# Score banks in pairs with one maximum per pair, the other products in four banks, and a planner that issues value sums and whole-array products in separate steps

## The chip, the core and the metric

The kernel runs on one core of one Trainium2 chip. The metric is the device time of one execution in microseconds. Three runs of the kernel before gave 1620.12, 1620.18 and 1624.03 us, median 1620.18 us. Engines are called PE (matrix products; PEld is its weight load), DVE (vector), ACT (activation), POOL (GpSimd) and SP (which here only issues DMAs).

## The reference

Input `x` is 32 sequences of 256 rows of 128 numbers. Each sequence goes through a pre-norm decoder layer and then a mixture-of-experts layer. The change lies in the attention of the decoder layer alone, so that is what must be seen:

```python
x = layer_norm(hidden_states, ln1_g, ln1_b)
q, k, v = jnp.split(x @ c_attn_w + c_attn_b, 3, axis=-1)
a = _attn_core(split_heads(q), split_heads(k), split_heads(v), causal_bool=True)      # 16 heads of 8
hidden_states = merge_heads(a) @ attn_proj_w + attn_proj_b + residual
x = layer_norm(hidden_states, lnx_g, lnx_b)
q = x @ q_attn_w + q_attn_b                                  # keys and values from the encoder rows
a = _attn_core(..., extra_bias=scorer_logits, tril_diag2_additive=True)
hidden_states = hidden_states + merge_heads(a) @ x_proj_w + x_proj_b
# then layer norm, a gelu MLP, layer norms with residuals, gate, 8 experts with top 2, a shared expert
```

`_attn_core` is softmax(q k / sqrt(8) + mask) v, with the row maximum subtracted.

## The kernel before, in words

There are 32 self attentions (s0 to s31) and 32 cross attentions (c0 to c31), one of each for every sequence. A head has only 8 numbers, so the scores are made in strips of 32 rows of the array: four groups g of four heads j, the group's operands in partitions 32g to 32g+31, and a number of q or k in three bf16 parts. Four matmuls, one for each strip, run at once, into four PSUM banks.

One attention has these pieces:

- `normed_in`: layer norm. For a self attention the input is normalised twice, to `xn` (which is multiplied later) and to `hs`, the residual in `h_all`; `moments` and both `normed` are DVE work, `rsqrt` (L190, L191) is POOL work.
- `turned`, `projections`, `values`: whole-array products with float32 operands. `projected` (L240) splits q and k into bf16 parts on POOL (L250 to L253), writes them to DRAM and reads them back in strip order (tiles `q`, `k`, then `qs`, `kr`), on the SP queue.
- `maxima` (L420): scores by query into banks `sc`, a quarter of the array rows each; DVE takes the negative maximum of each bank (L443). Its only purpose is the row maximum. `split` (POOL) makes three bf16 parts of the maxima, `turned_maxima` transposes them.
- `weights` (L477): scores by key, once more, with the maximum added as a product, into banks `st`; ACT takes exp to the tile `wt` (L503).
- `weighted` (L513): value sums `av`, which use 32 columns of the array at a time (128*32 in the profile); 64 matmul passes for most of them.
- `back`, `turned_back`, `joined`: transposes and the output product, whole-array again.

The order on PE is written out by hand. Time is counted in half steps. A self attention takes 6 half steps by query and 6 by key, a cross attention 8 and 8; the keys start LAG = 13 half steps after the queries. A planner in the kernel's Python places each attention, and each extra piece at a half step. Then a loop goes through pairs of half steps (called a step below): `issue` mixes the score products of the step by query and by key over the four strips, then come the maxima and exps, then the extras of the step, with `weighted` last. Thus PE does a block of score products, then the extras, then the next block. Within a block the first half fills `sc` of two groups and `st` of the other two, the second half the reverse. The order of the other engines is left to a scheduler at build time.

All PSUM tiles come from one ring of eight banks (tag `ps`, L159 to L162): a step's four `sc`, four `st` and its extras in turn. A product waits until the bank that it gets was read: an `sc` bank by DVE's maximum, an `st` bank by ACT's exp, an extra's bank by its copy.

The planner's function `full(step, cost, ...)` puts a piece at a step, or one later when the step has more than 1.9 of cost; `weighted` goes through it too, so a step may hold value sums and whole-array products. AHEAD = 7 bounds how many self attentions may run ahead of the cross attentions. After attention come a stage of norms and MLP and the experts' stage, with the same ring of eight banks.

Of the kernel before, what the change touches and what calls it, by code (L numbers as in the profile page):

```python
# [27 lines left out]
LAG = 13  # L28
V_BUFS = 4
QK_BUFS = 4  # L30
AHEAD = 7


COLS = ["ln1_g", "ln1_b", "lnx_g", "lnx_b", "ln2_g", "ln2_b", "bq", "bk", "bqx", "bkx", "bv", "bvx"]
# [10 lines left out]
def transformer_moe_kernel(ctx: ExitStack, tc: tile.TileContext, ins, out: bass.AP):  # L45
# [152 lines left out]


    with ExitStack() as actx:  # L200
        wk = actx.enter_context(tc.tile_pool(name="wk", bufs=3))
        wl = actx.enter_context(tc.tile_pool(name="wl", bufs=5))
        wtp = actx.enter_context(tc.tile_pool(name="wtp", bufs=22))
        kx = actx.enter_context(tc.tile_pool(name="kx", bufs=1))
        dram = actx.enter_context(tc.tile_pool(name="dram", bufs=1, space=bass.MemoryType.DRAM))

# [135 lines left out]
        class Attention:  # L342
# [77 lines left out]
            def maxima(self, qb, js, gp):  # L420

                nk = S if qb else (P + 2 if self.cross else P)
                n = len(js)
                if qb not in self.ms:
                    self.ms[qb] = wl.tile([P, NG, NJ], F32, tag="m", name="m")
                m = self.ms[qb]
                work, tiles = {}, []
                for g in (2 * gp, 2 * gp + 1):
                    st = slice(32 * g, 32 * g + 32)
                    t3 = bank("sc")[:, 0 : n * nk].rearrange("p (c k) -> p c k", k=nk)  # L430
                    tiles.append((g, t3))
                    todo = [(nk, t3[:, c, :], self.qs[st, j, qb * P : qb * P + P], self.kr[st, j, part, 0:nk],
                             (c, part) == (0, 0)) for c, j in enumerate(js) for part in range(3)]
                    for a in range(5 if self.cross and not qb else 4):
                        k0 = qb * P + 32 * a
                        w = min(32, nk - k0)
                        todo.append((n * w, t3[:, :, k0 : k0 + w], eye_q[self.cross][st, a, :],
                                     tri_q[st, 0:w].unsqueeze(1).to_broadcast([32, n, w]), False))
                    work[g] = todo

                def after():
                    for g, t3 in tiles:
                        nc.vector.tensor_reduce(m[:, g, js[0] : js[0] + n], t3, AX.X, ALU.max, negate=True)  # L443
                return work, after

            def split(self, qb):
# [10 lines left out]
            def turned_maxima(self, qb):  # L457
                if qb == 0:
                    self.mT = wl.tile([P, S], BF16, tag="mT", name="mT")
                pt = ps.tile([P, P], BF16, tag="ps", name="pt_m")  # L460
# [16 lines left out]
            def weights(self, kb, js, gp):  # L477
# [107 lines left out]
        extra, filled = {}, {}  # L585

        def on(step, f, *args):
            extra.setdefault(step, []).append((f, args))

        def full(step, cost, f, *args):  # L590
# [4 lines left out]
            filled[e] = filled.get(e, 0) + cost  # L595
            on(e, f, *args)
            return e

        by_query, by_key, first, free = {}, {}, {}, {}
        at = begun = ended = 0
        cross = True
        while ended < NB:
            ready = ended < begun and first[ended] <= at
            cross = begun == NB or (ready and not cross) or begun - ended == AHEAD
            if cross:
                x = pairs[ended][1]
                at = max(at, first[ended])
                ended += 1  # L610
            else:
                x = pairs[begun][0]
                begun += 1

            at = max(at, *(free.get((x.cross, what, x.b % n), at) for what, n in (("qk", QK_BUFS), ("v", V_BUFS))))
            at += at % 2
            halves, keys = x.query_halves(), x.key_halves()
            s = at
            at += len(halves)
            if not x.cross:  # L620
                on(s - 22, x.load)
            on(s - 18, x.normed_in)
            if x.b < QK_BUFS:
                on(s - 17, x.spares)
            on(s + 2, x.biased)
            e = full(s - 14, 0.35, x.turned)
            e = full(e + 2, 0.5 if x.cross else 0.9, x.projections)
            assert e <= s - 8, (e, s)
            if not x.cross:
                full(e + 2, 0.55, x.values)  # L630
            for i, h in enumerate(halves):
                by_query[s + i] = (x, h)
            for qb in range(2):
                last = s + max(i for i, h in enumerate(halves) if h[0] == qb)
                on(last + 1, x.split, qb)
                e = full(last + 3, 0.13, x.turned_maxima, qb)
                assert e < s + LAG
            for i, h in enumerate(keys):
                by_key[s + LAG + i] = (x, h)
            end = s + LAG + len(keys)  # L640
            free[x.cross, "qk", x.b % QK_BUFS] = end + 14
            half = end if x.cross else s + LAG + sum(h[0] == 0 for h in keys)
            e = full(half + 1, 1.2 if x.cross else 0.9, x.weighted, 0)
            e = full(max(e, end + 1), 1.8, x.weighted, 1)
            free[x.cross, "v", x.b % V_BUFS] = e + 12
            e = full(e + 2, 0.5, x.back)
            e = full(e + 2, 0.25, x.turned_back)
            e = full(e + 2, 0.6, x.joined)
            first[x.b] = e + 20

        on(-18, spares)
        on(-15, diagonals)
        on(-13, max_frames, False)
        on(-11, picks)
        on(-9, out_biases)
        full(-5, 0.5, encoder_turned)
        on(-5, logit_parts)
        on(-4, encoder_rows)
        full(-2, 0.5, encoder_keys)
        full(0, 0.5, encoder_values)  # L660
        on(2, max_frames, True)
# [254 lines left out]

    def experts(c):
        rhs = xnT[:, c * CH * P : (c + 1) * CH * P]
        pw = ps.tile([P, P], BF16, tag="ps", name="pw")
# [98 lines left out]
```

## Time and profile before

One execution was profiled: its own time was 1619.44 us, with a span of 1617.7 us, so 1.7 us lie around the span.

| stretch of the span, us | what runs | PE busy, us | DVE busy, us | ACT busy, us | POOL busy, us | granted PE clock |
|---|---|---|---|---|---|---|
| 0 to 200 | start of attention | 134.4 | 121.7 | 78.2 | 104.7 | 0.85 |
| 200 to 960 | attention, steady | 677.6 | 535.4 | 486.2 | 346.8 | 0.99 |
| 960 to 1016 | end of attention | 47.8 | 27.4 | 32.8 | 10.7 | 0.98 |
| 1016 to 1204 | norms and MLP | 171.0 | 130.8 | 121.9 | 114.2 | 0.91 |
| 1204 to 1617.7 | experts | 405.0 | 231.8 | 93.7 | 39.7 | 0.99 |

Attention takes 63% of the span. The first block of scores starts at 34.7 us and the last attention product ends near 1014 us. A row of the profile's groups names the line, engine, operation and tiles, how often it ran, the total busy time, the mean of one in ns, and the idle time of the engine before it with what ended that idle time. "issue" there means that nothing that the profile shows ended it. A float32 matmul is two passes, and each counts as a matmul and a weight load.

### The profile page before, as it was taken

Reading aid. Unit: us, or ns where it says so; the run is one execution under the profiler, and the core shown is the slowest. Engines: PE = TensorE matmul, PEld = TensorE weight load, DVE = VectorE, ACT = ScalarE, POOL = GpSimd, SP = SyncE. Lnnn points to the kernel's source line nnn. Section 1 sums busy time; section 2 is a strip of 40 time slices with the busy share of each in tenths; the row PEclk is TensorE's granted clock in tenths of the full one; section 3 lists DMA queues with packets and bytes.
Section 4 is the critical chain, followed back from the end, with each engine's and each line's share of the span. In section 5 each row is a group of like instructions: output and inputs, shape, how many; then the busy total and the mean of one; then the engine's idle time right before and its main releaser. Section 6 shows DMA issues by size and latency. Waiting matters only on the chain.

```text
span 1617.7 us, 74346 instructions
## 1 busy us (share of the span) xinstructions
PE 1435.8 (89%) x33116; PEld 1110.6 (69%) x33116; DVE 1047.0 (65%) x2749; ACT 812.7 (50%) x1824; POOL 616.1 (38%) x1443
## 2 busy tenths in 40 slices
PE   3677898998889888889898998799889999999997
PEld 2566677777777777777777777477655656565665
DVE  6647677676676776777666664477766464646564
ACT  1353566666666666666666565678532222222221
POOL 7444445444454444544444231687511010100101
PEclk8888899999999999999999999899979999999999
DMA  5632233232322322313232010600000000000000
GB/s 135 188 100 75 63 92 97 77 112 65 104 86 74 109 70 86 104 61 111 68 90 89 28 32 11 163 1 1 1 1 13 7 13 7 14 7 14 7 14 13
DMA packets 106033, 97.25 MB, mean 60 GB/s; under 512 B 4764, under 2 KB 105360, under 8 KB 105712
## 3 DMA queue, kind: packets, MB, share of 16 engines
q1 hardware_dynamic: 104432, 91.49, 18.4%
q8 instruction: 259, 4.24, 1.1%
q10 hardware_dynamic: 1280, 1.01, 0.2%
q14 instruction: 62, 0.51, 0.1%
HBM read 54.47 MB, written 37.77 MB: 57 GB/s over the span
## 4 chain that ended last, share of the span: by engine, by line
PE 68%; DVE 17%; POOL 5%; ACT 4%; issue 3%; DMA 2%; SPq 0%; POOLq 0%; ACTq 0%; DVEq 0%
DVE m L443 11%; PE av L525 11%; PE sc L580 9%; PE po L944 8%; PE pa L930 8%; PE pb L931 8%; PE st L580 7%; PE po L853 4%; PE pf L846 3%; PE pq L245 3%; ACT wt L503 2%; POOL r L191 2%; PE pc L937 2%; DVE st L182 2%; PE pa L541 1%
## 5 line engine op out<-in xcount | busy, mean ns | idle before, releaser
L443 DVE TENSOR_REDUCE m<-sc 128x2 f32<-128x512 f32 (+2 forms) x896 | 496.3, 608 | 236.9 <-PE sc L580 215.0
L503 ACT ACTIVATE wt<-st 128x512 f32<-128x512 f32 (+1 forms) x896 | 420.7, 539 | 256.3 <-PE st L580 196.8
L580 PEld LDWEIGHTS <-qs 32*128 32x128 bf16 x6144 | 225.2, 95 | 93.7 <-issue 80.5
L933 ACT ACTIVATE sa<-pa,cols 128x512 f32<-128x512 f32 x144 | 98.9, 687 | 308.5 <-PE pa L930 305.7
L580 PE MATMUL st<-mT,pick 32*128 32x256 bf16 (+2 forms) x2048 | 241.4, 244 | 5.1 <-issue 5.1
L190 POOL TENSOR_SCALAR r<-mv 128x2 f32<-128x2 f32 (+1 forms) x160 | 31.9, 199 | 501.9 <-DVE mv L183 434.3
L580 PEld LDWEIGHTS <-strips 32*128 32x128 bf16 x7424 | 189.3, 94 | 22.3 <-issue 18.8
L580 PE MATMUL sc<-kr,qs 32*128 32x128 bf16 (+1 forms) x3072 | 164.5, 250 | 33.3 <-DMA kr<-k 25.0
L580 PE MATMUL st<-qs,kr 32*128 32x128 bf16 (+1 forms) x3072 | 177.8, 247 | 10.2 <-issue 6.1
L580 PE MATMUL sc<-krx,qs 32*128 32x256 bf16 (+1 forms) x3072 | 178.9, 246 | 5.4 <-issue 3.5
L580 PE MATMUL st<-qs,krx 32*128 32x130 bf16 (+1 forms) x3072 | 176.7, 243 | 4.8 <-issue 3.5
L930 PE MATMUL pa<-h_all,w 128*128 128x512 f32 x288 | 149.4, 601 | 0.0
L931 PE MATMUL pb<-h_all,w 128*128 128x512 f32 x288 | 147.9, 595 | 0.0
L580 PE MATMUL sc<-strips 32*128 32x64 bf16 (+2 forms) x3840 | 140.3, 193 | 6.2 <-issue 5.8
L580 PE MATMUL st<-strips 32*128 32x64 bf16 (+2 forms) x3584 | 136.3, 192 | 9.1 <-issue 8.9
L944 PE MATMUL po<-w,h 128*128 128x128 f32 x1152 | 141.6, 277 | 0.0
L944 PEld LDWEIGHTS po<-w,h 128*128 128x128 f32 x1152 | 134.9, 192 | 7.7 <-issue 7.7
L525 PE MATMUL av<-wt,vpadx 128*32 128x128 f32 (+1 forms) x4096 | 111.7, 253 | 31.9 <-DVE m L443 28.2
L191 POOL TENSOR_TENSOR r<-r,nhalf 128x2 f32<-128x2 f32 (+1 forms) x160 | 133.2, 838 | 9.9
L580 PEld LDWEIGHTS <-kr 32*128 32x128 bf16 x3072 | 117.0, 94 | 19.1 <-issue 16.5
L525 PEld LDWEIGHTS av<-wt,vpadx 128*32 128x32 f32 x4096 | 98.3, 112 | 43.9 <-DVE m L443 36.2
L934 DVE SCALAR_TENSOR_TENSOR h<-pb,cols,sa 128x512 f32<-128x512 f32 x144 | 107.7, 749 | 31.9 <-PE pb L931 28.2
(163 smaller groups left out, 2624.5 us busy)
## 6 DMA issues: line engine op xcount, KB each, us to landing
kr<-k SPq DMA_DIRECT2D x32, 768.0 KB
k<-qkp SPq DMA_DIRECT2D x32, 576.0 KB
qs<-q SPq DMA_DIRECT2D x64, 256.0 KB
q<-qkp SPq DMA_DIRECT2D x64, 192.0 KB
x<-in_x_dram SPq DMA_DIRECT2D x32, 128.0 KB
x_all<-in_x_dram SPq DMA_DIRECT2D x8, 512.0 KB
out_dram<-y SPq DMA_DIRECT2D x16, 256.0 KB
w<-in_rw_dram SPq DMA_DIRECT2D x1, 1024.0 KB
```

The costliest lines, as they stand in the source:

```text
L191: nc.gpsimd.tensor_tensor(r, r, nhalf[:, 0:n], ALU.pow)
L245: nc.tensor.matmul(pq[:, i * S : i * S + S], lhsT=w, rhs=xT, start=True, stop=True)
L443: nc.vector.tensor_reduce(m[:, g, js[0] : js[0] + n], t3, AX.X, ALU.max, negate=True)
L503: nc.scalar.activation(w[:, 0 : n * nq], t, AF.Exp)
L525: nc.tensor.matmul(av[32 * g : 32 * g + 32, j // 2, to : to + n], lhsT=self.vp[:, kb, g, WINDOW[j] : WINDOW[j] + 32], rhs=self.wts[kb, g, ...
L580: nc.tensor.matmul(dst, lhsT=lhsT, rhs=rhs, start=start, stop=False, skip_group_check=True)
L853: nc.tensor.matmul(po[:, i, :], lhsT=self.g[:, f, i * P : (i + 1) * P], rhs=wmlp[:, f, :], start=f == 0, stop=f == FF // P - 1)
L930: nc.tensor.matmul(pa, lhsT=w1[:, e, 0:D], rhs=rhs, start=True, stop=True)
L931: nc.tensor.matmul(pb, lhsT=w1[:, e, D : 2 * D], rhs=rhs, start=True, stop=True)
L933: nc.scalar.activation(sa, pa, AF.Silu, bias=col(C_B1 + 2 * e))
L934: nc.vector.scalar_tensor_tensor(h[:, e, :], pb, col(C_B1 + 2 * e + 1), sa, ALU.add, ALU.mult)
L944: nc.tensor.matmul(po[:, i, :], lhsT=h[:, e, i * P : (i + 1) * P], rhs=w2[:, e, :], start=e == 0, stop=False)
```

## The change

- **Banks.** In attention, two rings take the place of one: `sc` tiles are now pairs of banks, two pairs in all (four banks), and everything else (`st`, `av`, transposes, projections) shares four banks. A ring of eight is opened again after attention.
- **Maximum.** One DVE maximum reads a pair (two groups) where two read one bank each: 448 operations for 896.
- **Norm of a self attention.** The two reciprocal roots are made in one power operation of four columns on POOL where two had two columns each; the residual `hs` is normalised on POOL, not DVE.
- **Exp tiles.** The ring of 22 tiles of 512 columns becomes 18 of 512 and 8 of 260.
- **Planner.** `full` now chooses the cheapest of several steps within a reach; a step that holds a value sum is dear to it, and value sums are placed by `columns` without regard to cost. The plan is made four times, each time with the last round's value-sum steps. AHEAD is 8, preparation begins 28 and 24 half steps ahead for 22 and 18, and buffers count as free sooner.

The diff, cut to its core:

```diff
-AHEAD = 7
+AHEAD = 8
+SOON = 2
...
-    ps = ctx.enter_context(tc.tile_pool(name="ps", bufs=8, space=PSUM))
-    def bank(name):
-        return ps.tile([P, 512], F32, tag="ps", name=name)
+    rings = {}
+    def bank(name, dtype=F32, n=512):
+        return rings["ps"].tile([P, n], dtype, tag="ps", name=name)
...
+        rings["sc"] = actx.enter_context(tc.tile_pool(name="ps_sc", bufs=2, space=PSUM))
+        rings["ps"] = actx.enter_context(tc.tile_pool(name="ps_a", bufs=4, space=PSUM))
-        wtp = actx.enter_context(tc.tile_pool(name="wtp", bufs=22))
+        wtp = actx.enter_context(tc.tile_pool(name="wtp", bufs=1))
...
-                    r1 = rsqrt(wk, mv, 1.0, EPS, "a")
-                    r2 = rsqrt(wk, mv, 1.0 + EPS, EPS * EPS, "b")
+                    r = wk.tile([P, 2, 2], F32, tag="rab", name="r")
+                    nc.gpsimd.tensor_scalar(r[:, 1, :], mv[:, :, 1], 1.0 + EPS, EPS * EPS, ALU.mult, ALU.add)
+                    nc.gpsimd.tensor_scalar(r[:, 0, :], mv[:, :, 1], 1.0, EPS, ALU.mult, ALU.add)
+                    nc.gpsimd.tensor_tensor(r, r, nhalf.rearrange("p (a b) -> p a b", b=2), ALU.pow)
+                    r1, r2 = r[:, 0, :], r[:, 1, :]
                     for t in range(2):
                         normed(self.xn[:, t, :], xs[t], mv, r2, t)
-                        normed(self.hs[t], xs[t], mv, r1, t)
+                        nc.gpsimd.tensor_scalar(self.hs[t], xs[t], mv[:, t, 0:1], r1[:, t : t + 1],
+                                                ALU.subtract, ALU.mult)
...
+                t4 = rings["sc"].tile([P, 2, 512], F32, tag="sc", name="sc")[:, :, 0 : n * nk].rearrange(
+                    "p g (c k) -> p g c k", k=nk)
                 for g in (2 * gp, 2 * gp + 1):
-                    t3 = bank("sc")[:, 0 : n * nk].rearrange("p (c k) -> p c k", k=nk)
+                    t3 = t4[:, g % 2]
...
-                    for g, t3 in tiles:
-                        nc.vector.tensor_reduce(m[:, g, js[0] : js[0] + n], t3, AX.X, ALU.max, negate=True)
+                    nc.vector.tensor_reduce(m[:, 2 * gp : 2 * gp + 2, js[0] : js[0] + n], t4, AX.X, ALU.max, negate=True)
...
-                        w = wtp.tile([P, 512], F32, tag="wt", name="wt")
+                        cols, bufs = (512, 18) if n * nq > 260 else (260, 8)
+                        w = wtp.tile([P, cols], F32, tag=f"wt{cols}", name="wt", bufs=bufs)
...
-            e = step + step % 2
-            if filled.get(e, 0) + cost > 1.9 and filled.get(e + 2, 0) < filled.get(e, 0):
-                e += 2
+                def price(e):
+                    return max(0, filled.get(e, 0) + cost - 2.3) + 0.5 * (e in taken) + 0.02 * (e - step)
+                e = min(range(step + step % 2, max(step + step % 2, step + reach) + 1, 2), key=price)
...
+            def columns(step, f, *args):
+                e = step + step % 2
+                own.add(e)
+                on(e, f, *args)
+                return e
...
-            at = max(at, *(free.get((x.cross, what, x.b % n), at) for what, n in (("qk", QK_BUFS), ("v", V_BUFS))))
+                at = max(at, free.get(qk, -99) + 10)
...
-            free[x.cross, "qk", x.b % QK_BUFS] = end + 14
+                free[qk] = end + 1
-            e = full(half + 1, 1.2 if x.cross else 0.9, x.weighted, 0)
-            e = full(max(e, end + 1), 1.8, x.weighted, 1)
+                e = columns(half + 1, x.weighted, 0)
+                e = columns(max(e + 2, end + 1), x.weighted, 1)
...
-            first[x.b] = e + 20
+                first[x.b] = e + (26 if x.b >= SOON else 16)
...
+    rings["ps"] = ctx.enter_context(tc.tile_pool(name="ps", bufs=8, space=PSUM))
```

In the steady part the plan repeats every 14 half steps (seven steps, one self and one cross attention). Before, the seven steps hold: four steps with one value sum each, three of these with whole-array products ahead of it (`turned`; `back`, two `turned_maxima` and `projections`; `turned_back`), and three steps with whole-array products alone. After, four steps hold one value sum each (one of these with a `turned_maxima`), and three hold all else: step A two `back`, two `turned_maxima`, `values` and `turned`; step B two `turned_back`, `projections` of a cross attention and `turned`; step C two `joined`, a `turned_maxima` and `projections` of a self attention. Over the whole plan, 90 steps mix a value sum with whole-array products before and 36 after.

More of the change, by code (lines that the diff above doesn't have):

```diff
@@ L426, in maxima @@
                 m = self.ms[qb]
-                work, tiles = {}, []
+                work = {}
+                t4 = rings["sc"].tile([P, 2, 512], F32, tag="sc", name="sc")[:, :, 0 : n * nk].rearrange(
+                    "p g (c k) -> p g c k", k=nk)
                 for g in (2 * gp, 2 * gp + 1):
                     st = slice(32 * g, 32 * g + 32)
-                    t3 = bank("sc")[:, 0 : n * nk].rearrange("p (c k) -> p c k", k=nk)
-                    tiles.append((g, t3))
+                    t3 = t4[:, g % 2]
                     todo = [(nk, t3[:, c, :], self.qs[st, j, qb * P : qb * P + P], self.kr[st, j, part, 0:nk],
@@ L459, in turned_maxima @@
                     self.mT = wl.tile([P, S], BF16, tag="mT", name="mT")
-                pt = ps.tile([P, P], BF16, tag="ps", name="pt_m")
+                pt = bank("pt_m", BF16, P)
                 nc.tensor.transpose(pt, self.mp[qb].rearrange("p g r -> p (g r)"), ident_b)
@@ L584, in transformer_moe_kernel @@
         pairs = [(Attention(b, False), Attention(b, True)) for b in range(NB)]
[L585 to L590, printed above, removed]
-            e = step + step % 2
-            if filled.get(e, 0) + cost > 1.9 and filled.get(e + 2, 0) < filled.get(e, 0):
-                e += 2
[L595 to L613, printed above, removed]
-            at = max(at, *(free.get((x.cross, what, x.b % n), at) for what, n in (("qk", QK_BUFS), ("v", V_BUFS))))
[L616 to L640, printed above, removed]
-            free[x.cross, "qk", x.b % QK_BUFS] = end + 14
-            half = end if x.cross else s + LAG + sum(h[0] == 0 for h in keys)
-            e = full(half + 1, 1.2 if x.cross else 0.9, x.weighted, 0)
-            e = full(max(e, end + 1), 1.8, x.weighted, 1)
[L645 to L648, printed above, removed]
-            first[x.b] = e + 20
@@ L651, in transformer_moe_kernel, with planned, on, full @@
[L651 to L661, printed above, removed]
+        def planned(taken):
+            extra, filled, by_query, by_key, first, joined, free = {}, {}, {}, {}, {}, {}, {}
+            def on(step, f, *args):
+                extra.setdefault(step, []).append((f, args))
+            def full(step, cost, f, *args, reach=10):
+                def price(e):
+                    return max(0, filled.get(e, 0) + cost - 2.3) + 0.5 * (e in taken) + 0.02 * (e - step)
+                e = min(range(step + step % 2, max(step + step % 2, step + reach) + 1, 2), key=price)
+                filled[e] = filled.get(e, 0) + cost
+                on(e, f, *args)
[3 more added lines that the diff above has]
+                own.add(e)
+                on(e, f, *args)
+                return e
+            own = set()
+            at = begun = ended = 0
+            cross = True
+            while ended < NB:
+                ready = ended < begun and first[ended] <= at
+                cross = begun == NB or (ready and not cross) or begun - ended == AHEAD
+                if cross:
+                    x = pairs[ended][1]
+                    at = max(at, first[ended])
+                    ended += 1
+                else:
+                    x = pairs[begun][0]
+                    begun += 1
+                qk, v = (x.cross, "qk", x.b % QK_BUFS), (x.cross, "v", x.b % V_BUFS)
+                at = max(at, free.get(qk, -99) + 10)
+                at += at % 2
+                halves, keys = x.query_halves(), x.key_halves()
+                s = at
+                at += len(halves)
+                if not x.cross:
+                    on(s - 28, x.load)
+                lead = min(24, s - joined[x.b] - 2) if x.cross else 24
+                on(s - lead, x.normed_in)
+                if x.b < QK_BUFS:
+                    on(s - 23, x.spares)
+                on(s + 2, x.biased)
+                e = max(s - lead + 4, free.get(qk, -99) - 2)
+                e = full(e, 0.5, x.turned, reach=s - 10 - e)
+                e = max(e + 2, free.get(qk, -99))
+                e = full(e, 0.6 if x.cross else 1.1, x.projections, reach=s - 8 - e)
+                assert e <= s - 8, (e, s)
+                if not x.cross:
+                    full(max(e + 2, free.get(v, -99)), 0.55, x.values)
+                for i, h in enumerate(halves):
+                    by_query[s + i] = (x, h)
+                for qb in range(2):
+                    last = s + max(i for i, h in enumerate(halves) if h[0] == qb)
+                    on(last + 1, x.split, qb)
+                    e = full(last + 3, 0.13, x.turned_maxima, qb, reach=s + LAG - last - 4)
+                    assert e < s + LAG
+                for i, h in enumerate(keys):
+                    by_key[s + LAG + i] = (x, h)
+                end = s + LAG + len(keys)
+                free[qk] = end + 1
+                half = end if x.cross else s + LAG + sum(h[0] == 0 for h in keys)
+                e = columns(half + 1, x.weighted, 0)
+                e = columns(max(e + 2, end + 1), x.weighted, 1)
+                free[v] = e + 2
+                e = full(e + 2, 0.5, x.back)
+                e = full(e + 2, 0.25, x.turned_back)
+                e = full(e + 2, 0.6, x.joined)
+                joined[x.b] = e
+                first[x.b] = e + (26 if x.b >= SOON else 16)
+            on(-24, spares)
+            on(-21, diagonals)
+            on(-19, max_frames, False)
+            on(-17, picks)
+            on(-15, out_biases)
+            full(-5, 0.5, encoder_turned, reach=2)
+            on(-5, logit_parts)
+            on(-4, encoder_rows)
+            full(-2, 0.4, encoder_keys, reach=2)
+            full(0, 0.4, encoder_values)
+            on(2, max_frames, True)
+            return extra, by_query, by_key, own
@@ L662, in transformer_moe_kernel @@
+        own = set()
+        for _ in range(4):
+            extra, by_query, by_key, own = planned(own)
         with tc.manual_schedule(engines={mybir.EngineType.PE}):
@@ L918, in experts @@
         rhs = xnT[:, c * CH * P : (c + 1) * CH * P]
-        pw = ps.tile([P, P], BF16, tag="ps", name="pw")
+        pw = bank("pw", BF16, P)
         nc.tensor.transpose(pw, cwp[:, c * CH : (c + 1) * CH, :].rearrange("p t r -> p (t r)"), ident_b)
```

## The prediction

> **What bounds the kernel now.** I read the busy times by stretch first. From 200 to 960 us PE is busy 677.6 of 760 us, the next engine (DVE) 535.4, so PE's order sets the pace, and 82 us of PE idle are the most that better waits can give there. Then I read who waits for whom:
>
> ```profile
> POOL r L190 <- DVE mv L183: 434.3, 65, 22.2
> ...
> PEld L580 <- issue: 130.7, 333, 8.2
> ...
> DVE h_all L195 <- POOL r L191: 54.7, 25, 6.7
> ...
> PEld av L525 <- DVE m L443: 48.7, 71, 4.5
> ```
>
> Two things hold PE. The last two lines are one chain: DVE, in order, stands at the residual's norm until POOL's power operation is done; the maxima stand behind it; the value sum stands for the `sc` bank. The timeline has it at its worst:
>
> ```profile
> 174.51 1.37 POOL L191 TENSOR_TENSOR r<-r,nhalf 128x2 f32<-128x2 f32 x2
> 175.25 0.35 DVE L195 TENSOR_SCALAR h_all<-x,mv,r 128x128 f32<-128x128 f32 x1 [4.07 <-POOL r L191]
> 175.51 0.76 DVE L443 TENSOR_REDUCE m<-sc 128x2 f32<-128x260 f32 x2
> ...
> 175.99 0.44 PE L525 MATMUL av<-wt,vpad 128*32 128x128 f32 x4 [4.39 <-DVE m L443]
> ```
>
> The second is "issue", idle time inside the score blocks that nothing shown ends. Its place tells what it is. The page counts 33116 matmuls and 33116 weight loads on PE, and 259 transfers of 4.24 MB on the instruction queue: 256 instructions and 16.4 KB for each. In the trace's order the "issue" gaps recur at the same place modulo 256, about 1.4 us after such a transfer ends. Windows from one gap's end to the next, 252.22 and 716.78 us on, show it; set beside them are one cycle's four value-sum steps and its three other steps (after the stretch: its span, then PE, PEld, DVE, ACT, POOL busy with their counts, granted clock, DMA share and GB/s):
>
> ```profile
> 252.22:255.96 3.74, 3.25 (x130) 2.78 (x130) 2.41 (x5) 1.46 (x3) 1.82 (x7) 1.00 0.02 4
> 716.78:720.53 3.75, 3.19 (x128) 2.77 (x128) 2.59 (x6) 1.46 (x3) 1.34 (x6) 1.00 0.03 7
> 564.86:583.87 19.01, 17.59 (x650) 15.08 (x651) 13.14 (x34) 11.58 (x26) 10.10 (x24) 0.95 0.06 18
> 583.87:592.20 8.33, 8.26 (x299) 7.21 (x296) 6.42 (x17) 6.67 (x19) 3.08 (x12) 1.00 0.72 231
> ```
>
> PE cannot pass 256 instructions in less than some 3.75 us (over 71 boundaries with such a gap the way to the next usable page is 3.46 to 4.18 us in the middle eight tenths, median 3.74). The four value-sum steps hold 1301 instructions in 19.01 us, 3.74 us per 256; the other three 3.58 us. The whole cycle already runs close to the instruction supply. Of the 82 us idle, 40 lie at these page boundaries and 42 are waits for banks and data.
>
> Here a rule is weighed. The Trainium skill, "Runtime: NRT & Kernel Launch", section "Instruction fetch mechanics", has blocks of 16 KiB and calls the cost of crossing one mostly hidden. The block size agrees; "hidden" does not: the gap before 716.79 us is 1.36 us. By the rule, all 82 us could go (1538 us); by the rows only the waits that do not turn into refill gaps. I take the rows.
>
> **The change, part by part.** Sums are against the profiled execution, 1619.4 us (0.8 below the median).
>
> Maximum per pair: 512 columns take 683 ns, 260 take 422, so 1.04 ns a column and 0.15 fixed. A pair of 512 should take 1.21 us for 1.37, a pair of 260 0.69 for 0.84: 448 x 0.15 = 69 us less DVE work. No row shows a read over two banks; without the saving it is 0, with a stumble between banks perhaps 0.15 each the other way. DVE is not the bound, so all count as nothing on the path: cover is DVE's idle, 225 us in the steady stretch.
>
> Residual norm to POOL: 64 operations leave DVE (0.40 us each) and its 54.7 us standing goes. POOL takes 64 of perhaps 0.3 us (between 0.2, a cast of 16 columns, and 0.67, a two-input operation of 256; the cast of 256 is 0.40), 19 us, and saves 32 x (2 x 0.705 - 1.04) = 12 us of powers. POOL is half idle in a steady cycle (14 of 28 us), so this is nothing too.
>
> Own rings: the value sum's bank is now the one that ACT's exp of the block's first half left, done some 0.2 us before the block ends (0.6 us each, 0.5 apart). So the 35 us or so that the steady stretch loses at `av`, `pt_x` and `pt_m` to DVE's maxima, and most of the remaining 7, go.
>
> What takes their place, step by step in a steady cycle, which now takes 28.7 us on average (755 us for 26.3 cycles; 19.9 for the value-sum steps, 9.0 for the others by the starts of their blocks):
>
> Value-sum steps: 1298 instructions, 5.07 pages. PE's own time would be 14.4 us (four blocks of 1.88, value sums 1.1 + 1.68 + 0.81 + 1.68, switches of 0.12 to 0.34), 2.8 us per 256, well under 3.75. So refill is the bound: four pages at 3.75 and the rest at its own pace, 18.0 us. At 3.6 it is 17.4, at 3.9 18.6.
>
> Steps A, B, C: blocks 1.74 + 1.47 + 1.54, products 3.5, switches 2.1, all from start to start in the trace: 10.3 us for 2.5 pages, so no refill gap, but the whole-array work that used to lie under refill in the value-sum steps now lies open. Waits on the ring of four are new. In A the third and fourth extra need exps of the block's second half, at about 0.8 and 1.3 us after the block; `values` waits for the copy of a `turned_maxima`, and the next block's first `st` for `values`' two copies: 0.75 us, by ACT rows of 0.5, 0.3 and 0.3. In C the block waits for the two `aT` copies and the `xT`: 0.45. Bounds: 0 if ACT is early, 2.4 if DVE's reads of both `back` come in between. I take 1.2: 11.5 us.
>
> Sum 29.5 for 28.7: +0.8 us a cycle, over 25.6 cycles +20 us, between -26 (no bank waits, 3.6 us pages: 27.7) and +51 (2.4 of waits: 30.7).
>
> Switches: "TensorEngine Tiling (Array Packing)", section "Key Properties", says that a change of tiling mode drains PE, which speaks for issuing value sums apart. The trace prices it: from the last whole-array product to the first value sum 0.34 us, from score block straight to value sum 0.12. 90 - 36 = 54 mixed steps fewer give 54 x 0.22 = 12 us by the rule; in the sum above they count as nothing, since those steps wait for instructions anyway.
>
> Start, 0 to 200 us: PE stands 4.4 us (above), 3.7, 2.4 and 1.9 us behind DVE's maxima, of which I take 11 back. The projection of s2 moves ahead of the first block (it ran at 36.6 us behind it); PE stood 8.0 us at 61.3 us for its `kr`. I take 8. With fewer holes the clock (0.85 here) should be held down less: 6. Together -25; bounds -38 and -5. The six half steps that AHEAD = 8 puts first add no work.
>
> End: 234 steps with scores for 238, and 21 not full for 30: -3, between -8 and +3. Exp tiles: cross attention needs eight small ones and releases them before the next asks; nothing, or at worst some us at the end. Loads 28 half steps ahead pass SP's other issues at no wait, since SP waits for POOL, not the reverse. The stages after attention are the same: 0 +- 3.
>
> Total: +20 - 25 - 3 = -8: 1611.4 profiled, 1612 as the median.
>
> **The rivals.**
>
> Refill gives way: pages at 3.6 us, no bank waits: -26 - 28 = -54, 1566 us. For it: the smallest page times are 3.3 to 3.5. Against: 3.75 in both windows.
>
> Four banks too few (slower): ACT holds both whole-array steps up, as `values`, `projections` and exps share four banks. Place: steps A and C. Price 2.4 us a cycle, +51 - 28 = +23, 1643 us. It decides from 1.5 us of bank waits a cycle (18.0 + 10.3 + 1.5 is 1.1 over 28.7, and 1.1 x 25.6 = 28 is what start and end give back). For it: ACT is the busiest evacuator there (6.67 of 8.33 us). Against: it is idle in the value-sum steps.
>
> Start bound by transfers: a self attention moves 192 + 576 + 256 + 768 KB by the page's list of DMAs, 1.8 MB; from 40 to 80 us 191 GB/s flowed, so 9.4 us each, and eight come at the head instead of six. If that is the limit, the start gives 0: 1637 us.
>
> No effect: the plan differs on nearly every step, so only a balance of the two halves gives it, within the first case.
>
> **How the numbers follow.** What a measurement can tell from no change is about 0.3%, 4.9 us. Likeliest, 1612 and its own range 1598 to 1624: chance 0.47, of which 0.34 faster and 0.13 the same. Refill gives way, 1566: 0.12, faster. Four banks: 0.28, slower. Transfers: 0.13, of which 0.02 the same and 0.11 slower. Faster 0.46, same 0.15, slower 0.39. The range 1582 to 1648 leaves out the far half of the second and the far part of the third case.
>
> **What would show it.** Right: `av` waits for ACT or nothing, no `h_all` wait on DVE; "issue" gaps of PE grow above 130 us and sit in steps D to G (the value-sum steps); steps A to C take some 11.5 us for 9.0; s2's `kr` wait is gone; maximum of 128x1024 near 1.21 us. Wrong: page times under 3.6 us, waits of `st` and `pa` on ACT above 60 us, or the first 200 us holding no more work than before.

## The result and the profile after

The changed kernel takes 1691.46 us (median of 4 runs, 1688.82 to 1699.02) against 1622.11 us for the kernel before (4 runs): a ratio of 1.0424, 95% interval 1.0372 to 1.0477. It is 69 us slower; 1612 us, 8 us faster, was predicted, and the range ended at 1648 us. The profiled execution took 1699.02 us with a span of 1697.1 us, 79.4 us over the span of before; it is the slowest of the four, 7.6 us over their median.

I cut both spans at equal amounts of score work. A full step, four half steps' worth of products, counts one; there are 224, and a steady cycle (one self and one cross attention) has seven. This table is worked out from the starts of the blocks in the two traces; "stops" are times without any matmul on PE, and the last column is the time in which the clock granted to PE was 0.50.

| stretch | before, us | after, us | predicted difference | PE stops before / after | clock at 0.50 before / after |
|---|---|---|---|---|---|
| span's start to 30 full steps | 210.9 | 212.9 | -25 | | |
| 30 to 200 full steps (24.3 cycles) | 698.8 | 772.3 | +20 | 76.6 / 118.8 | 3 / 79 |
| 200 to the end of attention | 103.7 | 107.6 | -3 | | |
| later stages | 604.2 | 604.3 | 0 | | |

So nearly all of it came in the steady part: 73.5 us, where 20 were predicted, and the gain forecast for the start is missing. These rows of who waits for whom in the kernel after answer to the four shown of before:

```profile
POOL r L192 <- DVE mv L185: 514.8, 59, 22.2
...
PEld L590 <- issue: 147.9, 344, 5.4
...
PEld L469 <- POOL mparts L461: 66.0, 27, 4.4
...
PE pt_m L469 <- POOL mparts L461: 62.1, 26, 4.3
...
DVE xn L197 <- POOL r L379: 23.7, 7, 9.3
```

The value sum's wait of 48.7 us for DVE's maxima is gone, as predicted. So is DVE's wait for the power at `h_all`, but in the first 124 us DVE still stands seven times for it, now at `xn` (the last row). The row that grew is this one of before:

```profile
PEld L461 <- POOL mparts L453: 7.8, 5, 2.1
```

PE stands for POOL's split of the maxima (L461 after) before their transpose `pt_m`; the two rows of after are the transpose's weight load and its matmul, one stop seen twice. By the trace's order some 22 of these stops, 55 us, lie ahead of one piece: the second `turned_maxima` of a cross attention. One of them, on PE (the score blocks' rows left out):

```profile
582.23 0.29 PE L469 MATMUL pt_m<-ident_b,mparts 128*128 128x128 bf16 x1 [2.71 <-POOL mparts L461]
582.45 3.24 PE L535 MATMUL av<-wt,vpadx 128*32 128x128 f32 x64
```

What POOL did meanwhile, back to back from 568.8 us on:

```profile
571.38 0.73 POOL L388 TENSOR_TENSOR h_all<-h_all,out_bias 128x256 f32<-128x256 f32 x1
...
573.07 0.67 POOL L257 TENSOR_TENSOR qkp<-qk,qkp 128x256 bf16<-128x256 f32 x1
573.70 1.01 POOL L379 TENSOR_TENSOR r<-r,nhalf 128x4 f32<-128x4 f32 x1
574.82 1.58 POOL L383 TENSOR_SCALAR h_all<-x,mv,r 128x128 f32<-128x128 f32 x2
576.49 0.73 POOL L388 TENSOR_TENSOR h_all<-h_all,out_bias 128x256 f32<-128x256 f32 x1
577.16 0.61 POOL L254 CAST qkp<-qk 128x512 bf16<-128x512 f32 x1
577.85 1.16 POOL L255 TENSOR_TENSOR qk<-qk,qkp 128x512 f32<-128x512 f32 x1
579.07 0.61 POOL L256 CAST qkp<-qk 128x512 bf16<-128x512 f32 x1
579.76 1.15 POOL L257 TENSOR_TENSOR qkp<-qk,qkp 128x512 bf16<-128x512 f32 x1
580.86 0.20 POOL L461 CAST mparts<-m 128x16 bf16<-128x16 f32 x1
```

The maxima to be split were there by 576.9 us, when DVE had done the two maxima of the block of 573.25 us. POOL, in order, first finishes the projections of a cross attention (256 columns) and of a self attention (512), which the new plan puts in the adjacent steps B and C, and between them the residual norm: 1.58 us for its two operations, 0.79 each. The five small operations of the split start at 580.86 and end at 582.2. In the steady part POOL's longest stretch without a pause over 0.3 us is 5.2 us in the trace of before and 15.7 us here. The slack is smaller too: in the plan of before this transpose stands two steps behind its split for 26 of the 32 cross attentions, in the new plan one step for all.

The stop costs more than its length. Windows of one cycle's value-sum steps, its steps A to C, and of the time before, in and after the stop (span, PE, PEld, DVE, ACT, POOL busy, granted clock, DMA share, GB/s):

```profile
573.25:595.38 22.13, 16.61 (x638) 14.11 (x638) 9.94 (x12) 10.48 (x22) 10.21 (x24) 0.92 0.33 107
595.38:606.61 11.23, 10.48 (x311) 8.85 (x309) 9.24 (x26) 8.05 (x23) 4.66 (x14) 1.00 0.06 16
578.20:579.80 1.60, 0.88 (x34) 0.58 (x28) 1.14 (x2) 1.12 (x3) 1.46 (x3) 1.00 0.02 4
579.80:582.20 2.40, 0.00 (x0) 0.00 (x0) 0.98 (x1) 0.92 (x2) 2.11 (x7) 0.90 0.20 71
582.20:585.00 2.80, 2.77 (x49) 2.48 (x53) 0.00 (x0) 0.27 (x1) 0.94 (x5) 0.50 0.93 311
```

After the stop PE runs at half clock for one stretch of 3.41 us, so the value sum of 64 passes takes 3.24 us; one of as many passes took 1.96 us at 559.13. Between 212 and 830 us, 15 of 19 stops of 2.1 us or more at this place are met by one or two such stretches. A stretch costs at most half its length, an estimate that takes PE to be busy at half speed all through it; the value sum above lost 1.28 of its 3.24 us. (The Trainium skill, "TensorE: Matmul & The Clock Gate", section "HAM oscillation — how this bites in real kernels", warns of PE gaps over some 3.4 us; here 13 of the 17 stops of 2.1 to 3.1 us were enough.)

Rows of DVE's groups by shape, one of before and two of after, show what came of the maxima:

```profile
L443 DVE TENSOR_REDUCE m<-sc 128x2 f32<-128x512 f32 x512 | 324.8, 683 | 133.1 <-PE sc L580 129.3 <-PE st L580 3.0
...
L451 DVE TENSOR_REDUCE m<-sc 128x4 f32<-128x1024 f32 x256 | 308.0, 1218 | 219.8 <-PE sc L590 211.2 <-PE st L590 6.9 <-POOL qkp L256 0.6
...
L451 DVE TENSOR_REDUCE m<-sc 128x4 f32<-128x520 f32 x128 | 88.7, 695 | 104.0 <-PE sc L590 79.9 <-PE st L590 21.4 <-POOL mparts L461 1.1
```

The time of one came out within 0.01 us: 1.21 us were predicted for the pair of 512 columns, 0.69 for the pair of 260. The saving did not. In the row of before 512 operations of 683 ns keep DVE busy for 324.8 us, not 350, because most maxima start some 0.08 us before the operation ahead of them ends. The busy time of all maxima fell from 496.3 to 469.3 us: 27 us, where 69 were predicted.

### The profile page after: what moved, and what is told of

The parts are those of the page before. It is cut to its first block, busy times and chain, and to the rows that moved or that the text cites. A ratio compares the mean times of both kernels' runs of the same rounds, so it can differ in the third digit from the quotient of the medians.

```text
span 1697.1 us, 73654 instructions
## 1 busy us (share of the span) xinstructions
PE 1469.1 (87%) x33100; PEld 1138.9 (67%) x33116; DVE 995.6 (59%) x2237; ACT 811.8 (48%) x1824; POOL 647.4 (38%) x1475
## 3 DMA queue, kind: packets, MB, share of 16 engines
q8 instruction: 259, 4.24, 1.1%
q10 hardware_dynamic: 1280, 1.01, 0.2%
## 4 chain that ended last, share of the span: by engine, by line
PE 63%; POOL 18%; DVE 7%; issue 6%; ACT 3%; DMA 2%; SPq 0%; POOLq 0%; ACTq 0%; DVEq 0%
PE av L535 11%; PE st L590 8%; PE po L976 8%; PE pa L962 8%; PE pb L963 7%; PE sc L590 7%; PE po L885 4%; PE pf L878 3%; ACT wt L513 3%; POOL h_all L383 3%; POOL qk L255 2%; POOL qkp L257 2%; POOL h_all L388 2%; DVE m L451 2%; POOL r L379 2%
## 5 line engine op out<-in xcount | busy, mean ns | idle before, releaser
L451 DVE TENSOR_REDUCE m<-sc 128x4 f32<-128x1024 f32 (+2 forms) x448 | 469.3, 1069 | 373.2 <-PE sc L590 331.7
L590 PE MATMUL st<-mT,pick 32*128 32x256 bf16 (+2 forms) x2048 | 258.3, 248 | 0.7 <-issue 0.7
L192 POOL TENSOR_SCALAR r<-mv 128x4 f32<-128x4 f32 (+1 forms) x96 | 18.8, 196 | 589.7 <-DVE mv L185 514.8
L590 PE MATMUL st<-qs,krx 32*128 32x130 bf16 (+1 forms) x3072 | 185.2, 244 | 20.6 <-issue 13.2
L590 PE MATMUL st<-qs,kr 32*128 32x128 bf16 (+1 forms) x3072 | 190.3, 254 | 6.9 <-issue 3.9
L590 PE MATMUL st<-strips 32*128 32x64 bf16 (+2 forms) x3584 | 143.7, 194 | 8.0 <-issue 8.0
L590 PEld LDWEIGHTS <-krx 32*128 32x128 bf16 x3072 | 119.5, 93 | 30.2 <-issue 26.3
L590 PEld LDWEIGHTS <-kr 32*128 32x128 bf16 x3072 | 129.9, 98 | 10.0 <-issue 9.5
L461 POOL CAST mparts<-m 128x16 bf16<-128x16 f32 x128 | 25.1, 196 | 289.9 <-DVE m L451 288.2
L535 PE MATMUL av<-wt,vpadx 128*32 128x128 f32 (+1 forms) x4096 | 128.6, 279 | 4.0 <-issue 2.3
L966 DVE SCALAR_TENSOR_TENSOR h<-pb,cols,sa 128x512 f32<-128x512 f32 x144 | 107.6, 749 | 31.4 <-PE pb L963 27.8
```

The source lines that it names most:

```text
L451: nc.vector.tensor_reduce(m[:, 2 * gp : 2 * gp + 2, js[0] : js[0] + n], t4, AX.X, ALU.max, negate=True)
L535: nc.tensor.matmul(av[32 * g : 32 * g + 32, j // 2, to : to + n], lhsT=self.vp[:, kb, g, WINDOW[j] : WINDOW[j] + 32], rhs=self.wts[kb, g, ...
L590: nc.tensor.matmul(dst, lhsT=lhsT, rhs=rhs, start=start, stop=False, skip_group_check=True)
L966: nc.vector.scalar_tensor_tensor(h[:, e, :], pb, col(C_B1 + 2 * e + 1), sa, ALU.add, ALU.mult)
```

## The experiments

Theory A: POOL's queue is the cause, through the split and the half clock behind each stop. Theory B: the ring of four, the pairs or the separated steps cost what the prediction's slower rival said, and the stop only shows where PE would stand anyway. B was later split in two, C (the plan) and D (the banks). Each ratio is to runs of the kernel before on the same chip: their median was 1620.07 us beside the runs on the transpose and the norm, 1614.86 beside those on plan and banks apart and the one-part maxima without the norm, and 1616.93 beside the undone pairs and the last kernel. Between these groups ratios compare better than microseconds.

**The transpose one step later.** The stop is taken away without changing any engine's work:

```diff
-e = full(last + 3, 0.13, x.turned_maxima, qb, reach=s + LAG - last - 4)
+e = full(last + (5 if x.cross and qb else 3), 0.13, x.turned_maxima, qb, reach=s + LAG - last - (6 if x.cross and qb else 4))
```

> The kernel after, with one line of the plan changed: the second transpose of a cross attention's maxima (pt_m) is put one step later. No engine's work changes. Theory A (POOL's queue): in the kernel after PE stands 55 us, 22 times of some 2.6 us, for the split of those maxima, which POOL does behind two projections' splits, two residual norms and two biases; each such stop is followed by 3.4 us at half clock, some 1.7 us more. With 3 us more of slack most of that goes: 80 us less, of which instruction refill may take 10 to 30 back; 1610 to 1640 us expected. Theory B (four banks and separated value sums cost what the prediction's slower case said): the wait only moves to another product; not below 1675 us.

1654.92 us (1645.63 to 1660.7), ratio 1.0197 (1.0146 to 1.0247): 37 us less than the kernel after. The waits:

```profile
PEld L590 <- issue: 162.1, 357, 5.3
...
PEld L469 <- POOL mparts L461: 10.6, 5, 4.0
...
PE pt_m L469 <- POOL mparts L461: 9.8, 5, 3.9
```

The stops of the steady part are gone, and the half clock there fell from 79 to 20 us. But 55 us of stops and at most 29 of half clock (half of 59) gave only 38 us between 30 and 200 full steps (772.3 to 734.4): "issue" grew, and the blocks' stops from 42.5 to 61.2 us. PE, no longer held, ran into the refill more often: stops at a page boundary rose from 64 to 95 (200 to 960 us), with medians of 3.78 and 3.88 us to the next usable page, against 71 and 3.74 before. A is right for half of the loss; 35 us to the kernel before stay, which A doesn't explain.

**The residual norm back on DVE, and twice on POOL.** Edits of the kernel after, one each:

```diff
-nc.gpsimd.tensor_scalar(self.hs[t], xs[t], mv[:, t, 0:1], r1[:, t : t + 1], ALU.subtract, ALU.mult)
+normed(self.hs[t], xs[t], mv, r1, t)
...
+for _ in range(2):
     nc.gpsimd.tensor_scalar(self.hs[t], xs[t], mv[:, t, 0:1], r1[:, t : t + 1], ALU.subtract, ALU.mult)
```

> The kernel after, with the residual norm of a self attention back on DVE (64 operations), the rest as it is. Theory A: 1.6 us less in POOL's queue each cycle (0.79 us an operation, where the prediction took 0.3): the pt_m wait falls from 2.5 to about 0.9 us, too short to lower the clock, and the first block starts some 4 us earlier: 1615 to 1645 us. Theory B: no gain; the old wait of DVE for POOL's power comes back instead, 1690 to 1710 us.

> The kernel after, with each residual norm done twice on POOL, to the same place. It adds 64 operations of 0.79 us to POOL and nothing to any other engine. Theory A: the pt_m wait grows by 1.6 us in each of some 22 cycles and the start by 3 to 5 us: 35 to 45 us more, 1725 to 1740 us. Theory B (POOL has room): within 10 us of the kernel after.

Twice on POOL: 1742.25 us, ratio 1.0752 (1.0723 to 1.078), some 51 us over the kernel after, where 35 to 45 were expected; in the profiled execution 31 more lie in the steady part and 16 more in the start. The wait followed the dose:

```profile
PEld L470 <- POOL mparts L462: 103.4, 27, 5.5
...
PE pt_m L470 <- POOL mparts L462: 99.0, 26, 5.4
```

Back on DVE: 1749.68 us, ratio 1.08 (1.0761 to 1.0838), 58 us slower than the kernel after, where 45 to 75 us less was expected. That expectation was wrong, and the waits say why:

```profile
PE sc L589 <- DVE m L450: 90.7, 37, 9.0
DVE h_all L197 <- POOL r L379: 86.8, 24, 4.1
```

One of 19 like it, on DVE:

```profile
566.84 0.25 DVE L185 BATCH_NORM_AGGREGATE mv<-st 128x2 f32<-128x6 f32 x2
571.14 0.60 DVE L197 TENSOR_SCALAR h_all<-x,mv,r 128x128 f32<-128x128 f32 x2 [4.05 <-POOL r L379]
571.65 2.35 DVE L450 TENSOR_REDUCE m<-sc 128x4 f32<-128x1024 f32 x2
```

The same queue, seen by another engine: POOL's power stands behind the projections' splits (at 570.08 in this trace), DVE stands for the power with two maxima queued behind, and with two score pairs in all PE stops at `sc` for 3.3 us at 569.65. So undoing the norm doesn't test Theory A alone, since it brings another wait for the same queue. The first block, though, starts at 33.4 us here and at 39.4 after: that delay comes with the norm on POOL. It does not follow the dose (38.1 us with the norm twice).

**The norm's part alone,** put into the kernel before:

> The kernel before, with only the norm's part of the change: one power operation of four columns, residual norm on POOL. Theory A: POOL's queue is longer by 1.6 us a cycle here too, but in this plan the two projections are not in adjacent steps and the split has slack, so little happens in the steady part; the first block starts 3 to 5 us later; 54 us of DVE's standing at the norm goes: 1610 to 1630 us. If the norm on POOL is harmful whatever the plan is: above 1650 us.

1622.97 us (12 runs), ratio 1.0016 (1.0002 to 1.003). In the profiled execution, the fastest of the twelve, the first block starts at 38.5 us instead of 34.7 and the steady part takes 691.9 us for 698.8: as expected, and next to nothing in the sum. POOL's longest stretch is 7.9 us here. The norm on POOL does harm beside a plan that crowds POOL, not by itself.

**Plan and banks apart.** Three kernels: the planner of before with all else of after; the late-transpose kernel with one ring of eight and a maximum per bank; and the late-transpose kernel with

```diff
-return max(0, filled.get(e, 0) + cost - 2.3) + 0.5 * (e in taken) + 0.02 * (e - step)
+return max(0, filled.get(e, 0) + cost - 2.3) + 0.0 * (e in taken) + 0.02 * (e - step)
```

> The kernel after, with the planner of before (AHEAD 7 too): the banks in pairs, the maximum per pair, the ring of four, the exp tiles and the norm on POOL stay. Theory C (the plan is what costs: whole-array products no longer lie under the instruction refill of the value-sum steps): 1600 to 1630 us. Theory D (the banks cost: two score pairs and a ring of four stop PE, whatever the plan): 1640 us or more, with waits of PE for DVE's maximum and ACT's exp.

> The kernel of the run with the late transpose (1655 us), with one ring of eight banks and a maximum per bank, as before; plan and norm as after. Theory C: 1650 to 1670 us, as the plan is the same and DVE has 69 us more to do beside it. Theory D: below 1640 us.

> The kernel of the run with the late transpose, with the planner's extra price for a step that holds a value sum set to 0: value sums and whole-array products share steps again (119 steps instead of 36). Banks, norm, AHEAD as after. Theory C: the whole-array products hide under the refill again: 1 to 1.5 us less in each of 25 cycles, 1615 to 1635 us. Theory D: no gain, or a loss where products wait in the ring of four: 1650 us or more.

All with the norm on POOL; the steady part is from 30 to 200 full steps of the profiled execution. These executions lie between 6.6 us under (the first cell) and 5.8 us over (the late transpose with pairs) the median of their kernel, so steady parts within some 10 us of each other are not told apart:

| plan | one ring of eight | pairs and ring of four |
|---|---|---|
| before | 1.0016 (1.0002 to 1.003), steady 691.9 us | 1.0229 (1.0198 to 1.0259), steady 720.0 us |
| after, late transpose | 1.0074 (1.0048 to 1.01), steady 711.9 us | 1.0197 (1.0146 to 1.0247), steady 734.4 us |
| after, late transpose, mixed | | 1.0213 (1.0178 to 1.0249), steady 724.8 us |

The banks cost 1.2 to 2.1% (20 to 34 us) with either plan, the plan little in the whole: D is right, C at most in part. (In the first row the rings of exp tiles differ as well; they are no cost, as ACT's waits for a value sum to free a tile are 17.7 us in the first cell and 0.4 in the second.) Mixing the steps again (1650.34 us) took 10 us off the profiled steady part, about 0.4 us a cycle where 1 to 1.5 was expected, and 10 off the start, and added 6 at the end; in the ratios, 1.0213 for 1.0197, no gain is left. With the ring of four, putting whole-array products back under the refill was worth nothing that these runs can tell. The value sums' weight loads wait there 42.1 us for exps, 13.5 us in the late-transpose kernel.

Where the ring holds PE is seen in two groups of weight loads, first with the ring of four (late-transpose kernel), then with the ring of eight, same plan:

```profile
L551 PEld LDWEIGHTS pa<-ident,avs 128*128 128x128 f32 x256 | 27.4, 140 | 12.3 <-ACT wt L513 9.6 <-issue 0.7
...
L290 PEld LDWEIGHTS pv<-wqkv,xT 128*128 128x128 f32 x128 | 18.4, 204 | 13.5 <-ACT mT L470 11.5 <-ACT wt L513 1.0 <-ACT aT L567 0.3
```

```profile
L549 PEld LDWEIGHTS pa<-ident,avs 128*128 128x128 f32 x256 | 27.9, 140 | 2.7 <-issue 1.5
...
L288 PEld LDWEIGHTS pv<-wqkv,xT 128*128 128x128 f32 x128 | 18.8, 207 | 1.6 <-issue 1.0
```

`back` waits for exps, `values` for the copy of a `turned_maxima`. Step A, which holds both, takes 4.88 us from block to block with the ring of four and 3.95 with the ring of eight. Over 24.3 cycles these 0.93 us make 22.6 us, as much as the two steady parts differ by (734.4 and 711.9). The second place is the end, where only score blocks by key are left and the four `sc` banks lie idle. The same six blocks, ring of four, then ring of eight:

```profile
1022.50:1043.20 20.70, 16.31 (x393) 12.82 (x391) 1.76 (x6) 9.62 (x26) 0.00 (x0) 0.75 0.01 3
```

```profile
1002.40:1014.20 11.80, 11.09 (x390) 9.07 (x388) 1.76 (x6) 9.09 (x26) 0.00 (x0) 1.00 0.02 5
```

With the ring of four the blocks by key have these four banks only, and PE stops for 0.5 to 0.7 us behind most of them until ACT has read one. 8.9 us are lost: by the rows 3.7 of them are time without a matmul, and 5.2 are longer products at a granted clock of 0.75 for 1.00.

**The pairs undone,** with the ring of four kept:

```diff
-        rings["sc"] = actx.enter_context(tc.tile_pool(name="ps_sc", bufs=2, space=PSUM))
+        rings["sc"] = actx.enter_context(tc.tile_pool(name="ps_sc", bufs=4, space=PSUM))
...
-                    nc.vector.tensor_reduce(m[:, 2 * gp : 2 * gp + 2, js[0] : js[0] + n], t4, AX.X, ALU.max, negate=True)
+                    for g, t3 in tiles:
+                        nc.vector.tensor_reduce(m[:, g, js[0] : js[0] + n], t3, AX.X, ALU.max, negate=True)
```

> The kernel of the run with the late transpose (1655 us), with the pairs undone: the scores by query have a ring of four single banks of their own and one maximum per bank; the other products stay in their ring of four. If the ring of four costs what the new banks cost (28 us between this plan with and without them), this run stays at 1650 to 1665 us. If the pairs do (a half block's two banks come free only together): 1625 to 1640 us.

1651.8 us, ratio 1.0214 (1.0175 to 1.0253), within the interval of the pairs (1.0197). The pairs, which take 26 us off DVE's busy time (1021.4 us without them, 995.6 with them), neither gain nor cost what these runs can tell; it is the split into two rings of four banks. The end takes 104.8 us here, without any half clock, against 96.9 with the ring of eight.

**Fewer instructions, and what helped put together.** In the kernel before, `for part in range(3)` of the maxima's products becomes `range(1)`; the second kernel adds the norm on POOL from the seventh sequence on.

> The kernel before, with the scores by query made from the first of the three bf16 parts of k only; the row maximum that is subtracted is then off by a rounding, which the division by the row's sum takes out again. 4096 of 33116 matmuls and as many weight loads go, 32 of 259 instruction blocks, 256 instructions a cycle. If PE is bound by instruction refill in the value-sum steps (3.75 us per 256) and by its own pace in the others: 2.1 and 1.2 us less a cycle, 3.3 x 32 = 105 us, 1510 to 1530 us. If neither is the bound and the waits for DVE and ACT are: less than 40 us.

> The kernel before with the two things that helped: maxima from the first part of k (1567 us), and the norm's part of the change from the seventh sequence on, so that POOL's queue at the start stays as before. The norm on POOL alone shortened the steady part by 7 us and lengthened the start by 4. If the same holds here: 1553 to 1563 us; as PE has more room beside the refill here, up to 20 us; if the waits of PE for DVE's maxima do not come from the norm: 1565 us or more.

The first took 1567.01 us, ratio 0.9703 (0.9681 to 0.9726): 48 us, between both expectations. The second took 1533.56 us (1532.15 to 1534.68), ratio 0.9478 (0.9446 to 0.951), faster than both kernels and than each of its expectations; the norm gave 2.3% (33 us) here, after nothing in the kernel before. The waits without it, then with it:

```profile
PEld av L525 <- DVE m L443: 57.8, 66, 2.8
DVE h_all L195 <- POOL r L191: 54.8, 25, 6.7
```

```profile
PEld av L536 <- DVE m L454: 16.9, 53, 0.8
...
DVE h_all L195 <- POOL r L191: 8.6, 1, 8.6
```

Taking away the refill's instructions or DVE's waits alone gives part of their length, both together more than the sum: 35 and 7 us in the steady part, against 69. (The whole times, 48 and 0 against 83, compare less well, since the norm alone was on POOL from the first sequence on.) I read this as refill and DVE's waits covering each other, but the clock has a share that no run takes apart: in the steady part it stood at 0.50 for 44 us in the first kernel and 14 us in the second, 3 in the kernel before.

## Why the prediction was wrong, point by point

Along the chain of kernels the 4.24% adds up: norm on POOL 0.16, plan 0.58, banks 1.23, transpose where the plan puts it 2.27. These are differences of ratios, each uncertain by about half a per cent, and they depend on the order: with the banks before the plan, the banks are 2.13 and the plan with its late transpose -0.32.

- **"POOL is half idle in a steady cycle (14 of 28 us), so this is nothing too": the step that failed.** It counted POOL's busy time over a cycle and not who is queued behind whom. The new plan puts both projections' splits in adjacent steps; with the norm between them POOL is busy for 13 us when a split that PE needs comes up behind them, one step before its transpose. Price: 37 us with the half clock, by the late transpose. The operation was mis-sized too: 0.82 us on average for "perhaps 0.3"; the nearest row by shape and operands was DVE's own 0.40, and POOL took twice that (the row below). The rival "waits on ACT" had its place elsewhere; none named POOL.

```profile
L383 POOL TENSOR_SCALAR h_all<-x,mv,r 128x128 f32<-128x128 f32 x64 | 52.2, 819 | 2.8
```

- **Half clock.** The prediction reckoned with the clock only at the start, as a gain. In the steady part 15 of 19 stops of 2.1 us or more brought one or two stretches of 3.4 us of it.
- **Steps A to C, 11.5 us, and bank waits of 1.2 us: right in the sum, in part by luck.** With the stop gone they take 11.7 us. The ring's part is 0.93 us in A for the predicted 0.75, but nearly nothing in C (3.70 us, 3.67 with the ring of eight) for 0.45, and B is shorter than with the ring of eight (3.07 for 3.34).
- **Value-sum steps, refill-bound at 18.0 us: right in kind, 0.7 us short.** With the stop gone four take 18.7 us. With A to C it makes 30.4 us a cycle for the predicted 29.5 and the 28.75 of before; the steady part as a whole is 36 us longer for the predicted 20, within the stated bound of +51.
- **"448 x 0.15 = 69 us less DVE work": mis-sized, without effect on the time.** It multiplied the times of single maxima, which overlap in the trace of before; 27 us of busy time went.
- **Switches, "12 us by the rule", counted as nothing: no run shows their price.** The 0.34 us runs from start to start and so holds the last product's own length, 0.27 us in most cases. The mixed plan has 119 such steps for 36; at 0.22 us each that would be 18 us more, and its ratio is 0.16% higher, which these intervals do not tell from nothing.
- **Start, -25: failed.** It came to +2. The wait for `kr` moved: none at s2, 5.2 us at 183 us. POOL, which the projections need, does ten operations of the residual norm (some 9 us) ahead of the first block, which started 4.7 us later. Without the separation price the start gave 9 us (201.7 for 210.9), so the plan's separation of steps accounts for some 10 of the 27 us that are missing; the rest is not taken apart.
- **End, -3 between -8 and +3: failed by the ring of four.** With one ring and the same plan it is -7 (96.9 for 103.7 us); the ring adds 12 in the late-transpose kernel, where the clock stood at 0.50 for 20 us of the end, and 8 in the one with single `sc` banks, where it never did.

What stays open: whether the plan alone is slower in the whole (0.58% with one ring, -0.32% with pairs and the ring of four, hardly over the intervals), and why the clock is low for 20 us from 49 us on in the kernel after, where no long stop precedes it.

## What to carry to other kernels

An engine with half of its time free is no cover for work that is queued in order: ask in which stretch the work lands, what stands behind it there, and which of these the bounding engine waits for. Banks that are split by use cannot lend each other room: price the ring in the stages where one side is idle. And where two limits may cover each other, as refill and DVE's waits seem to do here, the gain from removing one is read only after the other has been eased.

## What had not been expected of the hardware

- A POOL operation with one tensor input and two per-partition operands on 128x128 took 0.82 us on average, on DVE 0.40.
- PE stops of 2.1 to 3.1 us were followed by 3.4 us or more at half clock in 13 of 17 cases.
- A maximum over two PSUM banks shows no price at the bank's border: 1218 ns for 1024 columns, where the two shapes in single banks (683 ns for 512, 422 for 260) give 1213 by a fixed part and a price a column.
